# Channel attention's first group taken into the drain of the sublayer before it, and rows turned ahead of a chunk's last products

## The chip, the cores and the metric

The kernel runs on one core of a Trainium2 chip. The metric is device time in microseconds. A core has five engines with queues of their own[...]: TensorE (PE; its weight loads are shown as PEld), VectorE (DVE), ScalarE (ACT), GpSimd (POOL) and SyncE (SP), which here issues the transfers.

## The reference, cut to what matters

Four decoder layers run one after another over 64 sequences of 64 rows of 256 numbers, with a second stream `ctx` of the same shape. Each layer has an attention, a cross attention and a feed-forward sublayer, and after each comes a layer norm of the sum with what went in. The change touches the first layer and the edge to the second:

```
# first sublayer: causal attention, 16 heads of 16 that share one key and one value head
# second: channel attention (q = x, k = v = ctx), softmax over the channels of q
scaled = jnp.einsum('bsd,bse->bde', q, k) * scale        # scale = 1/16
attn = jax.nn.softmax(scaled, axis=1)
out = jnp.einsum('bde,bse->bsd', attn, v)
# third: feed-forward with 8-bit weights, hidden size 704
W = (wq - 128) * scale[:, None]
out = qlinear(silu(qlinear(x, gate)) * qlinear(x, up), down)
# second layer, first sublayer: needs the sum of 16 blocks of Wo (128 rows each)
```

## The kernel before, in words

The 4096 rows stand in eight groups of four tiles of 128 rows (`n_groups` = 8, `TG` = 4). `X[g]` holds a group's rows, `CT[g]` the transposed `ctx`; both stay on the chip. Layers are methods, called in turn by `run`; each opens its pools of on-chip buffers and closes them at its end. SP issues all loads (`load`, L327). The weights use a ring of eight buffers (`weight`), so that a load into a buffer waits for the last use of what was in it: `l1a` takes the place of the first sublayer's weights.

Within `manual_schedule` the program text fixes the order on PE, ACT, DVE and POOL. Outside it, and on SP always, a scheduler places the instructions.

`l0_attn` is the first sublayer. Its loop (`for i in range(n + 4)`) is a software pipeline over the 32 tiles. In step i come: `ended` for tile i-4 (sum with the residual L605, statistics L606 and L607, at a group's end rstd L228 and its power on POOL L230); `scores` of tile i (mask and products L539 and L544, maximum L553, subtraction L554); `probabilities` of tile i-1 (sum L563, reciprocal L564, division on POOL L565); `values` of tile i-3 (products L584, ScalarE's copy `ot` L589); one of four `parts` that prepare the next group (row turning with copies L488; keys and values L493 to L514; two query projections L493 with L530); `exponentials` of tile i (L558); `turned` for tile i-2 (transposes L236, copies L574); a piece of an earlier group's normalization, `behind` (L614, L618); `output` of tile i-3 (L595). The transposes of `turned` and the banks of the parts share two PSUM banks (tag `tr`); the scores have one buffer of four banks. The values v of a group are also exchanged between partition halves by two small transfers, vs<-v (L516), before POOL fills `vbd` with them (L526); POOL does this, and adds the bias to x (L521), in the query parts.

`l0_both` holds the other two sublayers. The feed-forward weights are loaded as integers and made into floats on DVE (L698). Each of eight chunks (one group) has HC = 6 units of 128 hidden columns. In unit u come `hidden` (gate and up products L795, Silu L797, product L798), `behind` (normalization L712, L714), then, for the tile of channel attention that the table `at` names, `divided` (reciprocal L757, division on POOL L762) and `scores` (products L738, maximum L742, scaling L743, exponentials L748), `down` for unit u-2 (L809), `values` for u-2 (L772, sum and statistics L725 to L727), and at a chunk's end `turn` of the next group's rows (transposes L785, copies L786: ScalarE the first half, VectorE the second). `at` gives tile (g, t) the unit 6(g-1)+t-2, so the loop starts at u = -8: group 0's four tiles run with no chunk beside them. `turn` and `hidden` share three PSUM banks (tag `gu`).

`l1_attn` loads the next weights; two sums over `l1_wo` (L868, L869, and their sum L870) stand in the text at its head.

## Time and profile before

| | |
|---|---|
| median of three runs | 4527.38 us (4523.95 to 4527.45) |
| profiled execution, own time | 4522.86 us |
| its span (first to last instruction) | 4521.2 us |
| granted TensorE clock, mean | 0.962 |
| first sublayer | until about 219.4 us of the span |
| group 0's channel attention | 219.4 to 252.6 us |
| first product of the first chunk | 260.58 us |
| last product of the last chunk | 619.5 us |
| the other layers | from there to 4521.2 us |

A profile is one execution, so sums are made against 4522.86 us. In rows of a timeline the columns are start, duration, engine, line and operation, out<-in, shape and count, and in brackets how long the engine had been idle and what released it. A row of waits names who waited for whom: microseconds in total, times, the longest. A row of stretches gives each engine's busy time, the granted clock, and the transfers' share.

### The profile page before, as it was taken

To read this page: it belongs to the slowest core of one execution; us is meant where nothing else is said; L and a number is where in the kernel's file an instruction comes from. 1 tells how busy PE (TensorE), PEld (TensorE's weight loads), DVE (VectorE), ACT (ScalarE), POOL (GpSimd) and SP (SyncE) were. 2 spreads that over 40 slices of the span, in tenths; PEclk is the share of its full clock that TensorE was granted. 3 is DMA by queue.
4 is the path that set the end of the run, shared out by engine and by line. 5 is a ranking of instruction groups with operands and counts; after the bars stand their busy time and mean duration, and the time that the engine had idled before them with its cause. 6 is when DMAs were issued, how large, how long until landed. Compare 5 with 4: busy or idle time off the path is not lost. (4 is left out here: it accounts for less than half of the span.)

```text
span 4521.2 us, 73893 instructions
## 1 busy us (share of the span) xinstructions
PE 4119.8 (91%) x28796; PEld 2664.4 (59%) x28816; DVE 3089.4 (68%) x6215; ACT 2020.6 (45%) x3669; POOL 1477.0 (33%) x1498
## 2 busy tenths in 40 slices
PE   8889988989988999839999999999979999999898
PEld 5644555666665555525666666666646666666566
DVE  6743435888765577767777777777756777777676
ACT  4645533766623566534444444444423332233343
POOL 4411111142331111105555555555523333333111
PEclk9989997999999999969999999999989999999999
DMA  4000011333300000011111111111220000000000
GB/s 142 13 21 2 3 42 33 64 80 71 75 1 21 1 1 1 10 47 27 26 29 28 26 29 24 29 29 27 59 63 10 10 10 10 10 10 13 6 16 17
DMA packets 99685, 128.26 MB, mean 28 GB/s; under 512 B 14916, under 2 KB 72452, under 8 KB 97928
## 3 DMA queue, kind: packets, MB, share of 16 engines
q1 hardware_dynamic: 99336, 123.53, 10.9%
q8 instruction: 228, 3.74, 0.4%
q14 instruction: 121, 0.99, 0.1%
HBM read 61.87 MB, written 19.42 MB: 18 GB/s over the span
## 5 line engine op out<-in xcount | busy, mean ns | idle before, releaser
L230 POOL TENSOR_TENSOR hrq<-hrq,neg_half 128x4 f32<-128x4 f32 x256 | 271.0, 1058 | 510.9 <-DVE hrq L228 510.8
L230 POOL TENSOR_TENSOR rstd<-rstd,neg_half 128x4 f32<-128x4 f32 (+1 forms) x168 | 148.4, 883 | 677.5 <-DVE rstd L228 595.1
L1054 DVE TENSOR_REDUCE mc<-sq 128x2 f32<-128x512 f32 x512 | 317.6, 683 | 68.3 <-PE sk L1052 66.2
L1060 ACT ACTIVATE e<-sk 128x512 f32<-128x512 f32 x512 | 265.8, 607 | 117.7 <-PE sk L1052 114.0
L230 POOL TENSOR_TENSOR hrk<-hrk,neg_half 128x4 f32<-128x4 f32 x160 | 187.9, 1174 | 290.0 <-DVE hrk L228 279.5
L1049 PE MATMUL sq<-l1x 32*128 32x256 f32 x2048 | 280.8, 412 | 1.6 <-DVE mc L1054 1.6
L1052 PE MATMUL sk<-l1x 32*128 32x256 f32 x2048 | 258.0, 399 | 0.0
L1556 PE MATMUL p<-l3a_wq,xt 128*128 128x512 f32 x512 | 244.4, 600 | 9.9 <-DVE v L217 9.9
L1556 PE MATMUL p<-l3x_wq,xt 128*128 128x512 f32 x512 | 236.2, 605 | 13.7 <-DVE k L1865 13.5
L1556 PE MATMUL p<-l3a_wk,xt 128*128 128x512 f32 x512 | 247.1, 605 | 0.0
L1049 PEld LDWEIGHTS sq<-l1x 32*128 32x128 f32 x2048 | 212.4, 197 | 55.5 <-issue 22.7
L1946 PE MATMUL acc<-l3x_wo,yt 128*128 128x256 f32 x1024 | 238.0, 385 | 0.7 <-ACT yt L215 0.7
L1556 PE MATMUL p<-l3a_wv,xt 128*128 128x512 f32 x512 | 234.4, 600 | 0.8 <-DVE k L217 0.4
L1763 PE MATMUL acc<-l3a_wproj,yt 128*128 128x256 f32 x1024 | 232.5, 380 | 0.0
L1763 PEld LDWEIGHTS acc<-l3a_wproj,yt 128*128 128x128 f32 x1024 | 194.8, 191 | 53.1 <-issue 29.2
L1946 PEld LDWEIGHTS acc<-l3x_wo,yt 128*128 128x128 f32 x1024 | 189.3, 190 | 28.3 <-ACT yt L215 0.9
L1052 PEld LDWEIGHTS sk<-l1x 32*128 32x128 f32 x2048 | 191.8, 190 | 7.0 <-issue 2.9
L1857 ACT ACTIVATE sq<-q 128x512 f32<-128x512 f32 x128 | 80.7, 631 | 206.5 <-DVE q L1865 153.9
L1556 PEld LDWEIGHTS p<-l3x_wq,xt 128*128 128x128 f32 x512 | 97.0, 195 | 125.2 <-issue 114.9
L1747 POOL TENSOR_TENSOR hry<-hry,neg_half 128x8 f32<-128x8 f32 x64 | 106.3, 1661 | 193.1 <-DVE hry L1743 193.1
L236 PEld LDWEIGHTS qT<-ident,q 128*128 128x128 f32 x1024 | 119.1, 141 | 77.2 <-issue 64.5
L1088 PE MATMUL ret<-e,vt 128*32 128x256 f32 x2048 | 140.0, 389 | 17.5 <-DVE mc L1054 16.6
(383 smaller groups left out, 10244.6 us busy)
## 6 DMA issues: line engine op xcount, KB each, us to landing
vs<-v SPq DMA_DIRECT2D x320, 128.0 KB
x<-in_x SPq DMA_DIRECT2D x8, 512.0 KB
ct<-in_ctxT SPq DMA_DIRECT2D x8, 512.0 KB
cn<-in_ctx SPq DMA_DIRECT2D x8, 512.0 KB
l1x<-in_ctx SPq DMA_DIRECT2D x128, 32.0 KB
l1x_x<-x SPq DMA_DIRECT2D x8, 512.0 KB
l1x<-l1x_x SPq DMA_DIRECT2D x128, 32.0 KB
l1x_r<-r SPq DMA_DIRECT2D x128, 32.0 KB
```

The lines of the kernel that those rows point to most:

```text
L230: nc.gpsimd.tensor_tensor(out, out, self.neg_half[:, :n], ALU.pow)
L236: self.nc.tensor.transpose(ps[:, j * P : (j + 1) * P], blk, self.ident)
L1049: nc.tensor.matmul(ps[:, n, :], x_[rows, j, part], c_[rows, j, :], start=True, stop=True)
L1052: nc.tensor.matmul(ps[:, n, :], c_[rows, j, part], x_[rows, j, :], start=True, stop=True)
L1054: nc.vector.tensor_reduce(mc[new % 2][:, ra + k, 2 * j : 2 * j + 2], ps, AX.X, ALU.max, negate=True)
L1060: nc.scalar.activation(es[rb + k], ps, AF.Exp, scale=scale)
L1088: nc.tensor.matmul(ret[32 * r : 32 * r + 32, :], vt[i % 2][:, lc, 4 * r + j, :], es[r][:, lc, :], start=lc == 0, stop=lc == 1,)
L1556: self.nc.tensor.matmul(ps, lhs(c), w(c, cols), start=c == 0, stop=c == 1 and bias is None)
L1747: nc.gpsimd.tensor_tensor(r, r, self.neg_half[:, :8], ALU.pow)
L1763: nc.tensor.matmul(acc[:, :D], yts[h % 2][:, h // 2, :], wp[n // 8][:, (n % 8) * D : (n % 8 + 1) * D], start=n == 0, stop=n == 15,)
L1857: nc.scalar.activation(sq, x, AF.Square)
L1946: nc.tensor.matmul(acc[:, :D], yts[h % 2][:, h // 2, :], wo[n // 8][:, (n % 8) * D : (n % 8 + 1) * D], start=n == 0, stop=n == 15,)
```

## The change

1. The functions of channel attention become a method, `channel_attention`, whose buffers the caller gives; the sum with statistics becomes `tile_sum`, the normalization `group_end`. The work of one tile is the same.
2. `l0_attn` loads `ctx` (`self.context(g)`, eight loads of 512 KB) at its own head. Its loop has two more steps, and runs the four tiles of group 0's channel attention in steps 32 to 37, in buffers of the first sublayer.
3. In that loop `turned` stands ahead of the parts and of `exponentials`, in every step.
4. In `l0_both`, group 1's tiles are at u = -1 to 2 (before: -2 to 1), the loop starts at u = -1, and `turn(0)` stands ahead of it. At a chunk's end `turn` stands in front of `down` and `values`, and VectorE makes both copies.
5. The loads for the next layer are issued in `l1_weights`, called in `l0_both`, and the two sums over `l1_wo` stand at u = 36 and u = 39.

On SP's queue the order of the eight `cn` loads and of the four vs<-v transfers of groups 0 and 1 is exchanged: the loads come first.

```
+    def tile_sum(self, state, g, t, z, a, b):
+        if t == 0:
+            state[g, "mv"] = self.smallp.tile([P, TG, 2], F32, tag="bnmv", name="bnmv", bufs=4)
+        st = self.smallp.tile([P, 6], F32, tag="bnst1", name="bnst1", bufs=4)
+        nc.vector.tensor_tensor(z[:, t, :], a, b, ALU.add)
+        nc.vector.bn_stats(st, z[:, t, :])
+        nc.vector.bn_aggr(state[g, "mv"][:, t, :], st)
+
+    def group_end(self, state, g, x, z, parts=1):
+        rstd, nb = self.small(TG, "rstd", bufs=4), self.small(TG, "nmr", bufs=4)
+        self.rsqrt(rstd, mv[:, :, 1], 1.0, 1e-5)
+        def apply(ts):
+            if ts[0] == 0:
+                nc.vector.scalar_tensor_tensor(nb, mv[:, :, 0], -1.0, rstd, ALU.mult, ALU.mult)
+            for i in ts:
+                nc.scalar.activation(
+                    x[:, i, :], z[:, i, :], AF.Identity, bias=nb[:, i : i + 1], scale=rstd[:, i : i + 1]
+                )
+        n = TG // parts
+        return [lambda i=i: apply(range(i * n, i * n + n)) for i in range(parts)]
+
+    def channel_attention(self, state, p_tile, vt_tile, z_tile, s_banks, o_bank):
...
...
     def l0_attn(self, ctx):
...
+        self.cns = [self.context(g) for g in range(self.n_groups)]
+        next_scores, next_divided, next_values = self.channel_attention(
...
-            for i in range(n + 4):
+            for i in range(n + TG + 2):
                 behind = ends.pop(0) if ends else None
-                if i >= 4:
+                if 4 <= i <= n + 3:
                     ended(*tiles[i - 4], state.pop((i - 4, "ps")))
                 if i < n:
...
                     state[i, "s"] = scores(g, t)
+                elif i < n + TG:
+                    next_scores(0, i - n)
                 if 1 <= i <= n:
                     probabilities(state[i - 1, "s"])
+                elif n < i <= n + TG:
+                    next_divided(0, i - n - 1)
                 if 3 <= i <= n + 2:
                     state[i - 3, "o"] = values(*tiles[i - 3], state.pop((i - 3, "pt")))
+                if 2 <= i <= n + 1:
+                    state[i - 2, "pt"] = turned(state.pop((i - 2, "s")))
                 if parts:
                     parts.pop(0)()
                 if i < n:
                     exponentials(state[i, "s"])
-                if 2 <= i <= n + 1:
-                    state[i - 2, "pt"] = turned(state.pop((i - 2, "s")))
                 if behind:
                     behind()
                 if 3 <= i <= n + 2:
                     state[i - 3, "ps"] = output(*tiles[i - 3], state.pop((i - 3, "o")))
+                if i >= n + 2:
+                    ends.extend(next_values(0, i - n - 2))
...
     def l0_both(self, ctx):
...
         def turn(g):
             xt = wk.tile([P, 2, NTOK], F32, tag="xt", name="xt")
-            for c, copy in enumerate((nc.scalar.copy, nc.vector.tensor_copy)):
+            for c in range(2):
...
-                copy(xt[:, c, :], ps)
+                nc.vector.tensor_copy(xt[:, c, :], ps)
...
-        at = {HC * (g - 1) + t - 2: (g, t) for g, t in tiles}
+        at = {HC * (g - 1) + t - (1 if g == 1 else 2): (g, t) for g in range(1, self.n_groups) for t in range(TG)}
+        self.l1_weights()
...
-            for u in range(min(at), len(units) + 2):
+            turn(0)
+            for u in range(-1, len(units) + 2):
...
                 if u in at:
                     scores(*at[u])
+                if u >= 0 and (u + 1) % HC == 0 and (u + 1) // HC < self.n_groups:
+                    turn((u + 1) // HC)
                 if u >= 2:
                     down(*units[u - 2])
                 if u - 2 in at:
-                    values(*at[u - 2])
-                if (u + 1) % HC == 0 and (u + 1) // HC < self.n_groups:
-                    turn((u + 1) // HC)
+                    ends.extend(values(*at[u - 2]))
+                if u in (HC * 6, HC * 6 + 3):
+                    self.l1_output_weight(u == HC * 6)
...
+    def l1_weights(self):
+        w = self.weight("l1a")
...
+    def l1_output_weight(self, first):
+        wo, half, raw = self.l1w[2:]
+        if first:
+            nc.vector.tensor_reduce(wo, raw[0], AX.X, ALU.add)
+        else:
+            nc.vector.tensor_reduce(half, raw[1], AX.X, ALU.add)
+            nc.vector.tensor_tensor(wo, wo, half, ALU.add)
```

More of the change, by code (lines that the diff above doesn't have):

```diff
@@ L433, in constants @@
             keep(rows, [[8, 4]], 7, -1, 0.0)
+    def tile_sum(self, state, g, t, z, a, b):
+        nc = self.nc
+        if t == 0:
[5 more added lines that the diff above has]
+    def group_end(self, state, g, x, z, parts=1):
+        nc, mv = self.nc, state.pop((g, "mv"))
+        rstd, nb = self.small(TG, "rstd", bufs=4), self.small(TG, "nmr", bufs=4)
[9 more added lines that the diff above has]
+        return [lambda i=i: apply(range(i * n, i * n + n)) for i in range(parts)]
@@ new lines, in channel_attention, with scores, divided, values @@
+    def channel_attention(self, state, p_tile, vt_tile, z_tile, s_banks, o_bank):
+        nc = self.nc
+        half = lambda b: slice(b * S, (b + 1) * S)
+        scale = 1.0 / 16.0
+        def scores(g, t):
+            x, cn = self.X[g], self.cns[g]
+            if t == 0:
+                state[g, "z"] = z_tile()
+            ps = s_banks()
+            for e in range(2):
+                for b in range(2):
+                    nc.tensor.matmul(
+                        ps[:, b, e, :], cn[half(b), t, e * P : (e + 1) * P], x[half(b), t, :], start=True, stop=True
+                    )
+            nb, sm = self.small(4, "nb4"), self.small(4, "sm4x")
+            nc.vector.tensor_reduce(nb, ps, AX.X, ALU.max, negate=True)
+            nc.vector.tensor_scalar_mul(nb, nb, scale)
+            p = p_tile()
+            for b in range(2):
+                for e in range(2):
+                    i = 2 * b + e
+                    nc.scalar.activation(
+                        p[:, b, e, :], ps[:, b, e, :], AF.Exp, bias=nb[:, i : i + 1], scale=scale,
+                        accum_out=sm[:, i : i + 1],
+                    )
+            state[g, t] = p, sm
+        def divided(g, t):
+            p, sm = state[g, t]
+            nc.vector.reciprocal(sm, sm)
+            vt = vt_tile()
+            src = self.CT[g][:, :, t * P : (t + 1) * P].rearrange("p e (b s) -> p b e s", b=2)
+            sums = sm.rearrange("p (b e) -> p b e", b=2)
+            for b in range(2):
+                nc.gpsimd.tensor_tensor(
+                    vt[:, b], src[:, b], sums[:, b].unsqueeze(2).broadcast_to([P, 2, S]), ALU.mult
+                )
+            state[g, t] = p, vt
+        def values(g, t):
+            p, vt = state.pop((g, t))
+            ps = o_bank()
+            for e in range(2):
+                for b in range(2):
+                    nc.tensor.matmul(ps[half(b), :D], vt[:, b, e, :], p[:, b, e, :], start=e == 0, stop=e == 1)
+            z = state[g, "z"]
+            self.tile_sum(state, g, t, z, ps[:, :D], self.X[g][:, t, :])
+            return self.group_end(state, g, self.X[g], state.pop((g, "z"))) if t == TG - 1 else []
+        return scores, divided, values
@@ L600, in ended @@
             xb, z = groups[g][3:]
-            if t == 0:
-                groups[g, "mv"] = self.smallp.tile([P, TG, 2], F32, tag="bnmv", name="bnmv", bufs=4)
-            mv = groups[g, "mv"]
-            st = self.smallp.tile([P, 6], F32, tag="bnst1", name="bnst1", bufs=4)
-            nc.vector.tensor_tensor(z[:, t, :], ps[:, :D], xb[:, t, :], ALU.add)
-            nc.vector.bn_stats(st, z[:, t, :])
-            nc.vector.bn_aggr(mv[:, t, :], st)
-            if t < TG - 1:
-                return
-            rstd, nb = self.small(TG, "rstd", bufs=4), self.small(TG, "nmr", bufs=4)
-            self.rsqrt(rstd, mv[:, :, 1], 1.0, 1e-5)
-            def shifts():
-                nc.vector.scalar_tensor_tensor(nb, mv[:, :, 0], -1.0, rstd, ALU.mult, ALU.mult)
-            def apply(t0):
-                for i in (t0, t0 + 1):
-                    nc.scalar.activation(
-                        self.X[g][:, i, :], z[:, i, :], AF.Identity, bias=nb[:, i : i + 1], scale=rstd[:, i : i + 1]
-                    )
-            ends.extend([shifts, lambda: apply(0), lambda: apply(2)])
+            self.tile_sum(groups, g, t, z, ps[:, :D], xb[:, t, :])
+            if t == TG - 1:
+                ends.extend(self.group_end(groups, g, self.X[g], z, 2))
         ends = []
@@ L626, in l0_attn @@
         n = len(tiles)
+        four = lambda a: a.rearrange("p r i k -> p (r i k)").rearrange("p (b e d) -> p b e d", b=2, e=2)
+        self.cns = [self.context(g) for g in range(self.n_groups)]
+        next_scores, next_divided, next_values = self.channel_attention(
+            {},
+            lambda: four(wk.tile([P, 4, 4, S], F32, tag="s", name="s", bufs=4)),
+            lambda: wk.tile([P, 4, P], F32, tag="pt", name="pt", bufs=4)[:, :2].rearrange("p b (e s) -> p b e s", e=2),
+            lambda: wk.tile([P, TG, D], F32, tag="z", name="z", bufs=2),
+            lambda: self.psum.tile([P, 4, 512], F32, tag="s", name="s", bufs=1)[:, :2].rearrange(
+                "p b (e d) -> p b e d", e=2
+            ),
+            lambda: self.bank("o", tag="ot", bufs=1),
+        )
         E = mybir.EngineType
@@ L676, in l0_both @@
         wk = ctx.enter_context(self.tc.tile_pool(name="l0b", bufs=2, reuse_waits="tile"))
-        cns = [self.context(g) for g in range(self.n_groups)]
-        half = lambda b: slice(b * S, (b + 1) * S)
-        scale = 1.0 / 16.0
         ws = []
@@ L703, in l0_both @@
         state, ends = {}, []
-        def ended(g, z):
-            mv = state.pop((g, "mv"))
-            rstd, nb = self.small(TG, "rstd", bufs=4), self.small(TG, "nmr", bufs=4)
-            self.rsqrt(rstd, mv[:, :, 1], 1.0, 1e-5)
-            def apply():
-                nc.vector.scalar_tensor_tensor(nb, mv[:, :, 0], -1.0, rstd, ALU.mult, ALU.mult)
-                for i in range(TG):
-                    nc.scalar.activation(
-                        self.X[g][:, i, :], z[:, i, :], AF.Identity, bias=nb[:, i : i + 1], scale=rstd[:, i : i + 1]
-                    )
-            ends.append(apply)
@@ L720, in sums @@
-        def sums(g, t, z, ps):
-            if t == 0:
-                state[g, "mv"] = self.smallp.tile([P, TG, 2], F32, tag="bnmv", name="bnmv", bufs=4)
-            st = self.smallp.tile([P, 6], F32, tag="bnst1", name="bnst1", bufs=4)
-            nc.vector.tensor_tensor(z[:, t, :], ps, self.X[g][:, t, :], ALU.add)
-            nc.vector.bn_stats(st, z[:, t, :])
-            nc.vector.bn_aggr(state[g, "mv"][:, t, :], st)
-        def scores(g, t):
-            x, cn = self.X[g], cns[g]
-            if t == 0:
-                state[g, "z"] = wk.tile([P, TG, D], F32, tag="z", name="z", bufs=3)
-            ps = self.psum.tile([P, 2, 2, D], F32, tag="s", name="s", bufs=1)
-            for e in range(2):
-                for b in range(2):
-                    nc.tensor.matmul(
-                        ps[:, b, e, :], cn[half(b), t, e * P : (e + 1) * P], x[half(b), t, :], start=True, stop=True
-                    )
-            nb, sm = self.small(4, "nb4"), self.small(4, "sm4x")
-            nc.vector.tensor_reduce(nb, ps, AX.X, ALU.max, negate=True)
-            nc.vector.tensor_scalar_mul(nb, nb, scale)
-            p = wk.tile([P, 2, 2, D], F32, tag="p", name="p", bufs=3)
-            for b in range(2):
-                for e in range(2):
-                    i = 2 * b + e
-                    nc.scalar.activation(
-                        p[:, b, e, :], ps[:, b, e, :], AF.Exp, bias=nb[:, i : i + 1], scale=scale,
-                        accum_out=sm[:, i : i + 1],
-                    )
-            state[g, t] = p, sm
@@ L754, in divided @@
-        def divided(g, t):
-            p, sm = state[g, t]
-            nc.vector.reciprocal(sm, sm)
-            vt = wk.tile([P, 2, 2, S], F32, tag="vt", name="vt", bufs=3)
-            src = self.CT[g][:, :, t * P : (t + 1) * P].rearrange("p e (b s) -> p b e s", b=2)
-            sums_ = sm.rearrange("p (b e) -> p b e", b=2)
-            for b in range(2):
-                nc.gpsimd.tensor_tensor(
-                    vt[:, b], src[:, b], sums_[:, b].unsqueeze(2).broadcast_to([P, 2, S]), ALU.mult
-                )
-            state[g, t] = p, vt
@@ L767, in values @@
-        def values(g, t):
-            p, vt = state.pop((g, t))
-            ps = self.bank("o", tag="o", bufs=1)
-            for e in range(2):
-                for b in range(2):
-                    nc.tensor.matmul(ps[half(b), :D], vt[:, b, e, :], p[:, b, e, :], start=e == 0, stop=e == 1)
-            z = state[g, "z"]
-            sums(g, t, z, ps[:, :D])
-            if t == TG - 1:
-                ended(g, state.pop((g, "z")))
+        scores, divided, values = self.channel_attention(
+            state,
+            lambda: wk.tile([P, 2, 2, D], F32, tag="p", name="p", bufs=3),
+            lambda: wk.tile([P, 2, 2, S], F32, tag="vt", name="vt", bufs=3),
+            lambda: wk.tile([P, TG, D], F32, tag="z", name="z", bufs=3),
+            lambda: self.psum.tile([P, 2, 2, D], F32, tag="s", name="s", bufs=1),
+            lambda: self.bank("o", tag="o", bufs=1),
+        )
@@ L817, in down @@
             for t in range(TG):
-                sums(g, t, z, acc[t // 2][:, t % 2, :])
-            ended(g, z)
-        tiles = [(g, t) for g in range(self.n_groups) for t in range(TG)]
+                self.tile_sum(state, (g, 1), t, z, acc[t // 2][:, t % 2, :], self.X[g][:, t, :])
+            ends.extend(self.group_end(state, (g, 1), self.X[g], z))
         units = [(g, i) for g in range(self.n_groups) for i in range(HC)]
-        at = {HC * (g - 1) + t - 2: (g, t) for g, t in tiles}
+        at = {HC * (g - 1) + t - (1 if g == 1 else 2): (g, t) for g in range(1, self.n_groups) for t in range(TG)}
+        self.l1_weights()
         E = mybir.EngineType
         with self.tc.manual_schedule(engines={E.PE, E.Activation, E.DVE, E.Pool}):
-            for u in range(min(at), len(units) + 2):
+            turn(0)
+            for u in range(-1, len(units) + 2):
                 behind = ends.pop(0) if ends else None
@@ L839, in l0_both @@
                 if u - 2 in at:
-                    values(*at[u - 2])
-                if (u + 1) % HC == 0 and (u + 1) // HC < self.n_groups:
-                    turn((u + 1) // HC)
+                    ends.extend(values(*at[u - 2]))
+                if u in (HC * 6, HC * 6 + 3):
+                    self.l1_output_weight(u == HC * 6)
             for part in ends:
                 part()
+    def l1_weights(self):
+        ins, DH = self.ins, 128
+        w = self.weight("l1a")
+        wkk = w[:, 0:256].rearrange("p (c n) -> p c n", c=2)
+        wvv = w[:, 256:512].rearrange("p (c n) -> p c n", c=2)
+        self.load(wkk, ins["l1_wk"].rearrange("(c p) n -> p c n", p=P))
+        self.load(wvv, ins["l1_wv"].rearrange("(c p) n -> p c n", p=P))
+        raw = []
+        for i in range(2):
+            r = self.weight(f"l1_wo{i}").rearrange("p (h n) -> p h n", h=8)
+            self.load(r, ins["l1_wo"][i * 8 * DH : (i + 1) * 8 * DH, :].rearrange("(h p) n -> p h n", p=P))
+            raw.append(r.rearrange("p h n -> p n h"))
+        self.l1w = wkk, wvv, w[:, 512:768], w[:, 768:1024], raw
+    def l1_output_weight(self, first):
+        nc = self.nc
+        wo, half, raw = self.l1w[2:]
[4 more added lines that the diff above has]
+            nc.vector.tensor_tensor(wo, wo, half, ALU.add)
     def l1_attn(self, ctx):
@@ L852, in l1_attn @@
         wk = self.pool(ctx, "l1a", 2)
-        w = self.weight("l1a")
-        wkk = w[:, 0:256].rearrange("p (c n) -> p c n", c=2)
-        wvv = w[:, 256:512].rearrange("p (c n) -> p c n", c=2)
-        wo = w[:, 512:768]
-        self.load(wkk, ins["l1_wk"].rearrange("(c p) n -> p c n", p=P))
-        self.load(wvv, ins["l1_wv"].rearrange("(c p) n -> p c n", p=P))
-        raw = []
-        for i in range(2):
-            r = self.weight(f"l1_wo{i}")
-            self.load(
-                r.rearrange("p (h n) -> p h n", h=8),
-                ins["l1_wo"][i * 8 * DH : (i + 1) * 8 * DH, :].rearrange("(h p) n -> p h n", p=P),
-            )
-            raw.append(r)
-        half = w[:, 768:1024]
-        nc.vector.tensor_reduce(wo, raw[0].rearrange("p (h n) -> p n h", h=8), AX.X, ALU.add)
-        nc.vector.tensor_reduce(half, raw[1].rearrange("p (h n) -> p n h", h=8), AX.X, ALU.add)
-        nc.vector.tensor_tensor(wo, wo, half, ALU.add)
+        wkk, wvv, wo = self.l1w[:3]
         bk, bv = self.column("l1_bk"), self.column("l1_bv_col")
```

## The prediction, made before the changed kernel ran

> **What bounds the kernel now.** I read the page's busy shares first, then busy time by stretches of the first layer (the only part whose instructions change place), then the waits of its second half, then single timelines at four places.

> ```profile
> ## 1 busy us (share of the span) xinstructions
> PE 4119.8 (91%) x28796; PEld 2664.4 (59%) x28816; DVE 3089.4 (68%) x6215; ACT 2020.6 (45%) x3669; POOL 1477.0 (33%) x1498
> ```

> TensorE is busy 91% of the span: a step pays only where TensorE waits. By stretches (us; PE, PEld, DVE, ACT, POOL busy; granted clock; DMA share, GB/s):

> ```profile
> 125.00:150.00 25.00, 23.99 (x367) 17.32 (x366) 20.82 (x33) 15.85 (x28) 11.91 (x11) 1.00 0.01 3
> ...
> 220.00:260.00 40.00, 19.09 (x94) 11.24 (x90) 21.36 (x47) 15.93 (x58) 7.03 (x12) 0.69 0.11 29
> ...
> 351.00:396.00 45.00, 41.35 (x157) 21.32 (x156) 17.66 (x45) 25.98 (x55) 5.18 (x9) 0.96 0.01 4
> ```

> The first sublayer's loop is full of TensorE work (24 of 25 us); channel attention of group 0 is a chain with TensorE busy 48% at clock 0.69; a chunk (45 us) loses about 4. The waits of the second half name it:

> ```profile
> PE gate L795 <- ACT xt L786: 21.9, 8, 3.7
> PE s L738 <- ACT p L748: 3.7, 2, 3.5
> ```

> Eight chunks, and the first product of each waits for ScalarE's copy of the turned rows. One boundary, from the timelines of PE, ACT and DVE:

> ```profile
> 397.50 1.04 PE L785 MATMUL xt<-ident,x 128*128 128x128 f32 x8
> 402.19 3.34 PE L795 MATMUL gate<-xt,l_wg 128*128 128x512 f32 x4 [3.66 <-ACT xt L786]
> 405.32 2.26 PE L795 MATMUL up<-xt,l_wu 128*128 128x512 f32 x4
> ...
> 401.54 0.59 ACT L786 COPY xt<-xt 128x512 f32<-128x512 f32 x1
> ...
> 396.94 1.19 DVE L742 TENSOR_REDUCE nb<-s 128x4 f32<-128x1024 f32 x1
> ...
> 398.57 0.69 DVE L786 COPY xt<-xt 128x512 f32<-128x512 f32 x1 [0.24 <-PE xt L785]
> ```

> The ACT copy takes 0.59 but stands behind four exponentials and their table load (398.43 to 401.54). VectorE's copy was done at 399.26. The products after the stall take 3.34 and 2.26, elsewhere 1.98 and 1.88 at full clock.

> **Gain 1, boundaries.** Chunks 1 to 5 stall 3.65, 3.66, 3.66, 3.66, 3.66 and lose 1.64, 1.74, 1.75, 0, 1.74 to the slower clock behind it: 25.1 us. With the change: scores end 395.67; four transposes, 0.5; the next four need the bank of the last gate, read by Silu until 396.22, so they end at 396.75 (0.1 waited); the down products (1.83) now lie behind them and end at 398.6. VectorE finishes its maximum at 398.33 and copies to 399.0 and 399.6. The gate starts with the first half, at 399.05: a wait of 0.45. Left: 0.55 a boundary, 2.7 in five. Gain 22.4. What is late next is VectorE's maximum ahead of the copies. Chunk 6 waits 0.24 plus hand-over: gain 0.4.
> [...] by the queues the 0.1 buys 3 us. I take the queues. [...]

> **Gain 2, the drain.** In before, the last subtraction of the first sublayer ends at 207.59 and the first chunk's gate starts at 260.58, up at 264.15. After, by before's durations: scores 1.1, maximum and scaling behind queued VectorE work, exponentials to 213.4; each next tile waits its round, ot copy 0.4, output 0.9, scores 1.1, maximum and scaling 1.65, exponentials 1.9 (about 5.95): 219.35, 225.2. Tile 3 also stands behind the last output, the first values and two sums (3 x 1.05): 233.3. Reciprocal and division 1.2, values 1.1, sums and rstd 1.3, power and shift 1.5, four applies 2.1 : 240.5. Turning and copying 1.8, group 1's maximum 1.3, dequantizing wg 1.9 and wu 1.9: gate 245.6, up 247.5. That is 16.6 earlier; some 8 us of this chain is TensorE's and the stretch it replaces ran at 0.69, so I take 2 off: 14.6. Bounds 11 and 16.6.
> In this the turning of group "-1" at 228.07 (the condition also held at u = -7) vanishes; it lay beside exponentials and is worth nothing by itself. The scale loads still wait for the last output (SP, behind l1a), and land some 10 us before they are used.

> **Chunk 0 and the moved sums.** Before:

> ```profile
> 288.87 3.68 DVE L869 TENSOR_REDUCE l1a<-l_wo 128x256 f32<-128x2048 f32 x1 [2.98 <-DMA l_wo<-in_l_wo]
> ...
> 301.55 2.08 PE L738 MATMUL s<-x,cn 64*128 64x256 f32 x8 [3.52 <-ACT p L748]
> ```

> The sum of l1_wo waits for its load in VectorE's queue; group 1's normalization and exponentials stand behind, and TensorE stalls 3.52, 1.2 more at the boundary, and loses 2.7 of clock: 7.4. After, the sums lie at u = 36 and 39, 3.7 and 4.1 us, in units of 6.9 and 6.4 us where VectorE has 3 to 5 of other work; only h products with two units of slack stand behind. I cost them at nothing (1 each if that slack is gone). But group 1 enters with one tile instead of two, so one more scores (1.1), and the loop exponentials, table load, Silu, product, maximum, table load takes 7.4 where TensorE has 4.7 to 6: waits 2.2, 1.6, 1.4; and turn(1) waits for group 1's applies, 2.1. Sum 8.4 against 7.6: 0.8 lost. With gain 2: 13.8.

> **Loss 1, the start.** In the changed order SP issues eight cn loads (0.5 MB each) before the first vs transfer, not after. The SP, POOL and PE timelines:

> ```profile
> 21.43 0.42 SPq L327 DMA_DIRECT2D l_ob<-in_l_ob  x1
> 22.84 4.42 SPq L516 DMA_DIRECT2D vs<-v  x4
> 28.15 9.19 SPq L327 DMA_DIRECT2D cn<-in_ctx  x8
> ...
> 31.77 2.34 POOL L521 TENSOR_TENSOR xb<-x,l_ob 128x1024 f32<-128x1024 f32 x1 [24.97 <-DMA vs<-v]
> ...
> 35.01 1.90 POOL L565 TENSOR_TENSOR s<-s,sm 128x1024 f32<-128x1024 f32 x1
> ...
> 36.97 1.97 PE L236 MATMUL pt<-ident,s 128*128 128x128 f32 x8 [9.15 <-POOL s L565]
> ```

> GpSimd waits for l_ob and vs, then fills vbd, then divides; TensorE stands 9.15 us. l_ob, issued behind seven open loads, took 10.3 us[...]. So vs waits for 4.2 MB more; at the 345 GB/s of 17 to 50 us, 12.2: it lands near 43.9 instead of by 31.8. The two vs copies and the last v copy follow (0.8), division at 44.9 instead of 35.01: 9.9 lost. Lower end: a small transfer overtakes, 0; upper end 12.2. I take 9.9 because l_ob is the nearest row. Turning tile 0 also moves ahead of the query projection at i = 2, which lay in that stall: its 1.8 comes out. Loss 11.7.

> **Loss 2, `turned` ahead of the parts, 25 tiles.** PE and POOL timelines:

> ```profile
> 115.48 0.66 PE L236 MATMUL pt<-ident,s 128*128 128x128 f32 x4 [0.34 <-ACT qT L530]
> ...
> 116.56 1.90 POOL L565 TENSOR_TENSOR s<-s,sm 128x1024 f32<-128x1024 f32 x1 [0.78 <-DVE sm L564]
> ...
> 122.31 1.90 POOL L565 TENSOR_TENSOR s<-s,sm 128x1024 f32<-128x1024 f32 x1 [3.03 <-ACT pt L574]
> ```

> Now the projection's bank is freed by ScalarE after the first half of `turned` (gaps 0.44, 0.44, 0.51, and 0 in the keys part). After, the projection waits for the first pt copy: 0.43 in each of four parts, so 0.3 lost a group. And `turned` needs the division: it is ready 6.28 after the values begin one tile earlier (117.99 to 124.27). TensorE's work until then is 6.37 with a projection between, 8.2 with keys, but 5.46 with the row turning: a wait of 0.8. Together 1.15 a group, 6.25 groups: 7.2. Ends: 2 (only the banks) and 31 (below).

> **Sum.** 22.4 + 0.4 + 13.8 - 11.7 - 7.2 = 17.7 us. The profiled execution took 4522.86 (span 4521.2), so 4505.2; the runs' median is 4.5 higher, so 4509.7.

> **Rivals.** (a) vs overtakes the cn loads, or lands early: loss 1 falls to 1.8, 4500. For it: a 16 KB transfer; against it: l_ob's 10.3. (b) VectorE is too late at the boundaries, so half the stall and the clock loss stay: gain 1 is 11, 4521. For it: its maximum ends only 0.3 before the down products; against it: the first copy suffices for the gate's first half. (c) Slower: the division decides in every tile, not one in four. `turned` stands directly behind it with 0.1 us to spare in projection tiles; if the wait is 0.8 plus 0.43 in each of 25 tiles, loss 2 is 31 and the time 4533. It decides from 1.0 us a tile (7.2 + 17.7, over 25).

> **How the numbers follow.** Forecast 0.60 (own range 4499 to 4519), (a) 0.14, (b) 0.15, (c) 0.11. A measurement of this kernel tells about 0.2% (9 us) from no change: below 4518.3 is faster, above 4536.4 slower. The forecast, nearly all of it, (a) and a part of (b) are faster: 0.75; the rest of (b) and most of (c): 0.19; 0.06 slower. Range 4495 to 4525.

> **What would show it.** vs landing at 43 to 45 and division of tile 0 near 45; PE waits of 0.4 on ACT pt and 0.8 on POOL s between 50 and 200; first gate near 266, 6 us after its old 260.58, because the two losses (18.9) come before gain 2's 13 to 15, and everything won after that; boundary gaps of 0.5 on DVE xt with gates at 1.98; the waits for ACT xt gone. The forecast is wrong if TensorE still stalls 2 us or more at boundaries, or if the loop's tiles grow by over 1 us.

## The result, and the profile after

The changed kernel takes 4507.9 us (median of 7 runs, 4501.6 to 4513.1), the kernel before beside it 4524.0 (7 runs, 4522.8 to 4527.6): a ratio of 0.9962, with a 95% interval of 0.9950 to 0.9973. That is 16.1 us faster; 17.7 were predicted, and a time of 4509.7. The profiled execution took 4513.13 us (span 4511.4). Up to the first products of the second layer (kv) it is 13.7 us ahead of the kernel before, and in the layers behind, whose instructions did not change, it gives 4.0 back.

How those 13.7 came about is seen by cutting both profiles at five events: POOL's division of tile 0, VectorE's last subtraction (tile 31), the first gate, the second chunk's first gate, the last chunk's. All numbers are lengths in us.

```
                               predicted   before    after   difference
start, to the division of tile 0    +9.9    35.01    44.42     +9.4
loop, to the last subtraction       +9.0   172.57   182.19     +9.6
drain, to the first gate           -13.0    52.99    43.17     -9.8
chunk 0                             -0.8    48.79    48.31     -0.5
chunks 1 to 6                      -22.8   274.53   252.18    -22.3
last chunk, to kv                    0      43.17    43.06     -0.1
sum                                -17.7   627.07   613.34    -13.7
```

The prediction counts the drain's 14.6 to the first `up` product (264.15 to 247.5, less 2). By its own times the gate in front of it comes 15.0 earlier, 13.0 with the 2 taken off; the other 1.6 lie behind the first gate, which would run at full clock, and so in the row of chunk 0 (+0.8 less 1.6). Five terms are within 0.6 us of the forecast; the drain is 3.2 off, and the first gate, foretold near 266, comes at 269.78. Now the lines. First the stretches (us; PE, PEld, DVE, ACT, POOL busy; granted clock; DMA share; GB/s) of the drain, of chunk 0 and of one later chunk:

```profile
228.00:270.00 42.00, 25.69 (x197) 15.39 (x186) 19.23 (x49) 16.57 (x51) 8.83 (x12) 0.80 0.10 28
269.70:318.00 48.30, 43.29 (x160) 21.60 (x161) 21.18 (x48) 29.11 (x65) 4.79 (x11) 0.93 0.07 22
360.00:405.00 45.00, 44.36 (x175) 23.65 (x175) 20.01 (x50) 28.32 (x62) 5.04 (x10) 1.00 0.07 24
```

The later chunk is full: 44.36 of 45 us, clock 1.00 (before: 41.35 at 0.96). The drain is not: clock 0.80. The waits of TensorE in the second half of the layer:

```profile
PE s L479 <- ACT p L489: 3.7, 2, 2.6
PE gate L808 <- DVE l_wg L777: 2.1, 1, 2.1
PE gate L808 <- DVE xt L799: 1.6, 5, 0.3
```

The 21.9 us for ScalarE's xt have become 1.6 for VectorE's. One boundary, from the timeline of PE:

```profile
400.52 1.89 PE L822 MATMUL acc<-l_wd,hid 128*128 128x256 f32 x8
402.74 1.99 PE L808 MATMUL gate<-xt,l_wg 128*128 128x512 f32 x4 [0.32 <-DVE xt L799]
```

A gap of 0.32 and a gate of 1.99, where there were 3.66 and 3.34. The start, from the timelines of SP and of POOL:

```profile
22.71 13.03 SPq L327 DMA_DIRECT2D cn<-in_ctx  x8
35.86 3.17 SPq L600 DMA_DIRECT2D vs<-v  x4
```

```profile
43.64 0.52 POOL L610 COPY vbd<-vs 64x64 f32<-64x64 f32 x2 [9.81 <-DMA vs<-v]
...
44.42 1.90 POOL L649 TENSOR_TENSOR s<-s,sm 128x1024 f32<-128x1024 f32 x1
```

vs is issued at 35.86 instead of 22.84, lands at 43.6, and the division follows at 44.42 instead of 35.01. And the loop's new waits, TensorE, 55 to 205 us:

```profile
PE prep L577 <- ACT pt L658: 5.5, 19, 0.3
PE pt L236 <- POOL s L649: 3.3, 6, 0.7
```

Both are the ones foretold, a little shorter each (0.29 for 0.43; five of the six divisions 0.61 or 0.65 for 0.8). A group of four tiles takes 24.90 us instead of 23.76: 1.14 more, where 1.15 were foretold.

### The profile page after: what moved, and what is told of

It is laid out like the page before. It is cut to its first block, busy times and chain, and to the rows that moved or that the text cites. A ratio compares the mean times of both kernels' runs of the same rounds, so it can differ in the third digit from the quotient of the medians.

```text
span 4511.4 us, 73874 instructions
## 1 busy us (share of the span) xinstructions
PE 4118.9 (91%) x28808; PEld 2662.9 (59%) x28808; DVE 3091.6 (69%) x6222; ACT 2018.8 (45%) x3662; POOL 1474.4 (33%) x1498
## 5 line engine op out<-in xcount | busy, mean ns | idle before, releaser
L1580 PE MATMUL p<-l3x_wq,xt 128*128 128x512 f32 x512 | 238.2, 609 | 13.9 <-DVE k L1889 13.7
L236 PEld LDWEIGHTS qT<-ident,q 128*128 128x128 f32 x1024 | 119.1, 141 | 77.3 <-issue 64.6
```

What stands on the lines that cost most here:

```text
L236: self.nc.tensor.transpose(ps[:, j * P : (j + 1) * P], blk, self.ident)
L1580: self.nc.tensor.matmul(ps, lhs(c), w(c, cols), start=c == 0, stop=c == 1 and bias is None)
```

## The experiments

Five questions: whether both losses come from where the working put them (four runs), what it is that gains at the boundaries (three), what the moved sums are worth (one), what the drain still leaves (three), and whether the clock is what a stall costs beyond itself (one). The lengths of the five stretches in each profiled execution, in us; start, loop, drain, chunk 0, chunks 1 to 6, and when kv begins:

```
                   start    loop   drain  chunk 0  chunks 1-6      kv
before             35.01  172.57   52.99    48.79      274.53  627.07
after              44.42  182.19   43.17    48.31      252.18  613.34
e1_vs_first        35.45  182.19   40.35    48.31      252.19  601.56
e2_turned_back     45.05  173.37   41.28    48.31      252.20  603.28
e3_both            35.00  172.60   40.37    48.33      251.87  591.24
e8_vs_act_queue    34.38  193.89   41.24    48.32      252.22  613.12
e4_copies_only     34.83  172.39   52.28    42.27      251.86  596.80
e5_front_only      34.72  172.73   52.97    48.34      274.13  625.97
e6_turn_both       34.30  172.28   52.29    42.56      251.31  595.81
e7_sums_only       34.31  172.71   52.99    45.05      276.17  624.40
e9_dequant_early   34.13  172.50   38.06    47.09      252.13  586.97
e10_two_ahead      36.00  172.23   38.69    44.20      251.94  586.13
e11_both_on_top    34.29  173.45   40.58    40.48      251.94  583.82
e12_filled         34.17  172.91   53.01    46.37      269.44  618.96
```

**e1: the loads of cn behind the first four transfers of vs (groups 0 and 1; not twelve, as the expectation has it).**

```
-        self.cns = [self.context(g) for g in range(self.n_groups)]
+                if i == 2:
+                    self.cns = [self.context(g) for g in range(self.n_groups)]
```

> The changed kernel with the eight loads of cn issued behind the twelve loads of vs of tiles 0 to 2 on SyncE's queue, instead of ahead of them. First theory (the loads of vs of tile 0 are served behind the 512 KB loads of cn in the order in which they were issued): the division of tile 0 goes back from 44.4 us to 35 us, everything up to the first gate comes some 9.4 us earlier, and the time is about 9.4 us below that of the changed kernel, near 4498 us. Rival (the division is late for another reason, x landing at 31 us or the bandwidth that all the loads share): it stays near 44 and the time near 4508 us. The first three scores would then wait for cn if cn came later than they do: a wait on cn at the first scores of a group of more than 1 us would show that.

4498.88 us, ratio 0.9947 (0.9934 to 0.9959). The start is back at 35.45, 9.0 us earlier, and no scores of group 0 wait for cn. It is the place of vs behind the cn loads that makes the start late; whether vs waits there to be served, as the expectation has it, or to be issued, e1 does not tell.

**e2: `turned` behind the exponentials again, but for the last six tiles (26 to 31; the expectation says four).**

```
-                if 2 <= i <= n + 1:
+                if n - TG <= i <= n + 1:
                     state[i - 2, "pt"] = turned(state.pop((i - 2, "s")))
...
                     exponentials(state[i, "s"])
+                if 2 <= i < n - TG:
+                    state[i - 2, "pt"] = turned(state.pop((i - 2, "s")))
```

> The changed kernel with the transposes of the probabilities (pt) of the tiles up to 27 behind the exponentials again, as before, and ahead of the parts only in the last four. First theory (the two short waits, 0.29 us on ACT pt and 0.61 us on POOL s, come of the new place and of nothing else): both go in the steady loop, the first gate comes some 7 to 9 us earlier, and the time is about 4499 us. Rival (the loop is bound by the division or the clock and the waits only change their place): the rate of the loop stays, and the time stays near 4508 us.

4502.77 us, ratio 0.9955 (0.9943 to 0.9968). The loop is 8.8 us shorter (182.19 to 173.37), and the first gate comes 10.1 earlier: the place of `turned` is the loss. Of that the median shows 3 us by the ratios, 5 by the times; the layers behind kv scatter by more than such differences, so the events up to kv carry these verdicts.

**e3: both.**

> The changed kernel with both edits: cn issued behind the first loads of vs, and pt turned behind the exponentials up to tile 27. If the two losses are separate and add up, the last subtraction comes back from 226.6 us to about 208 us, the first gate to about 251 us, and the time is about 19 us below the changed kernel, near 4489 us, 35 us below the kernel before. If they are the same wait seen twice, it is no more than 10 us below, near 4498 us.

4491.2 us, ratio 0.9931 (0.9917 to 0.9944). Start 35.00, loop 172.60, as before the change; the first gate is at 247.97, 21.8 us before that of the changed kernel (e1 alone 11.8, e2 alone 10.1). They add up: two losses. The waits of e3's loop, 55 to 205 us:

```profile
PE pt L236 <- ACT qT L614: 4.1, 12, 0.3
PE pt L236 <- POOL s L649: 2.9, 2, 1.7
```

Twelve short waits for a bank stand where the changed kernel has nineteen, and the division is waited for twice, not six times.

**e8: vs issued on ScalarE's queue.**

```
-                    nc.sync.dma_start(out=vs[half(b)], in_=v[half(1 - b)])
+                    nc.scalar.dma_start(out=vs[half(b)], in_=v[half(1 - b)])
```

> The changed kernel with the loads of vs issued on ScalarE's queue instead of SyncE's, at the same place of the program. First theory (vs waits only because it stands behind cn in one queue): vs of tile 0 lands within 4 us of its issue, the division of tile 0 is near 36 to 37 us, and the time is some 7 to 9 us below the changed kernel, near 4500 us. Rival (the transfers share one bandwidth, and vs is late whatever its queue): the division stays near 43 to 44 us and the time near 4508 us. [...]

4512.43 us, ratio 0.9979 (0.9970 to 0.9988): no better than the changed kernel, though the start is 34.38: vs is no longer what the division waits for. What it had waited for in the changed kernel is its turn to be issued on SP. It was issued 13.0 us later than before and was there 7.8 us after its issue (before, at most 8.9). e8 itself does not settle whether bandwidth matters too, for ScalarE issues group 0's vs at 12.91, ahead of the first cn load (24.89). What I had not seen is the price on ScalarE. Its timeline in e8, and below it the same place in e1:

```profile
138.05 1.45 ACT L584 ACTIVATE kbd<-prep,kbp,pair 128x512 f32<-128x512 f32 x2 [1.59 <-PE prep L577]
139.99 1.12 ACTq L600 DMA_DIRECT2D vs<-v  x2
141.16 1.06 ACT L642 ACTIVATE s<-s 128x1024 f32<-128x1024 f32 x1 [1.66 <-DVE z L443]
```

```profile
133.04 1.45 ACT L584 ACTIVATE kbd<-prep,kbp,pair 128x512 f32<-128x512 f32 x2 [1.59 <-PE prep L577]
134.38 1.05 ACT L642 ACTIVATE s<-s 128x1024 f32<-128x1024 f32 x1
```

The two issues take 1.12 us, and stand in ScalarE's order with the wait for v's copy in front of them, so the exponentials behind come 1.8 us later after `kbd`. From 83 us on a group takes 26.5 us instead of e1's 24.9, and 28.2 in the two that hold an interval of half clock (at 103 and 158 us); that is most of the 11.7 us by which the loop is longer than e1's. In the whole sublayer there are 16 such issues, of 0.55 us in the median. What ScalarE's queue spares vs is the place behind the 13.03 us of issues in SP's row above.

**e4, e5, e6: what gains at the boundary.** e4 is the kernel before with only this edit:

```
-            for c, copy in enumerate((nc.scalar.copy, nc.vector.tensor_copy)):
+            for c in range(2):
...
-                copy(xt[:, c, :], ps)
+                nc.vector.tensor_copy(xt[:, c, :], ps)
```

e5 is the kernel before with only `turn` moved in front of `down` and `values`; e6 has both edits.

> The kernel before with VectorE making both copies of xt, and the turn left behind the down products. First theory (the stall of 3.66 us and the clock that follows it come of ScalarE's copy, which stands behind the exponentials; with VectorE the copies follow the transposes at once): the gate waits about 0.9 to 1.3 us at each of the five boundaries on DVE xt, granted clock back at 1.00, some 3.9 to 4.5 us a boundary, 18 to 21 us in all: about 4504 us. Rival (the order in front of the down products does it): within 2 us of 4524 us.

> The kernel before with the turn in front of the down products of a chunk's last step, and its two copies on ScalarE and VectorE as before. First theory (the stall is fixed by ScalarE's copy behind the exponentials of the last step): the gates of the next chunk begin where they did or at most 1 us earlier, since the down products now lie behind the transposes and take 1.9 us of the wait; the clock may stay up since the idle gap is shorter than 3.66 us, which would be worth up to 1.7 us at four of the boundaries. So 4515 to 4524 us. Rival (the place does it, whatever engine copies): the stall goes and the time is near 4504 us.

> The kernel before with the turn in front of the down products and both copies on VectorE, and nothing else of the change. First theory: the gain of the six boundaries alone, 22.3 to 22.8 us, gate waiting 0.3 us on DVE xt at the granted clock 1.00: about 4501 us, so below the changed kernel, of which the other parts together lose some 7 us. Rival (the turns gain less without the early gate): near 4508 us or above.

e4: 4493.52 us, ratio 0.9932 (0.9919 to 0.9944). e5: 4522.44, 0.9994 (0.9986 to 1.0002), no difference. e6: 4494.09, 0.9934 (0.9920 to 0.9947). So VectorE's copy is all of it, and the place of the turn nothing. The gate of the same boundary in e4, PE, right behind the turn:

```profile
386.53 1.98 PE L795 MATMUL gate<-xt,l_wg 128*128 128x512 f32 x4 [0.45 <-DVE xt L786]
```

and what TensorE waits for in e5 between 300 and 560 us:

```profile
PE gate L795 <- ACT xt L786: 18.6, 6, 3.5
```

In e5 the start of the gate is set by ScalarE's queue, whatever TensorE does meanwhile. e4 also gained more than expected, and that in chunk 0, which is 6.5 us shorter. The stretches of chunk 0 in e4 and, below, in the kernel before:

```profile
259.50:301.70 42.20, 38.43 (x152) 19.74 (x152) 23.11 (x39) 22.31 (x49) 5.00 (x10) 1.00 0.18 54
```

```profile
260.50:309.30 48.80, 43.85 (x152) 22.47 (x152) 22.69 (x37) 24.13 (x52) 4.99 (x10) 0.87 0.16 47
```

The same 152 products take 38.43 us at clock 1.00 instead of 43.85 at 0.87, though a wait for ScalarE's p of 3.0 is still there (3.5 before). Of the 6.5 us, 5.4 are TensorE's time for the same work, and so the clock.

The size of e4 matters for the whole change. By itself it is some 14 us faster than the changed kernel, and e3, the changed kernel with both losses taken out, has nearly the same ratio (0.9931 against 0.9932; in the profiles kv comes 5.6 us earlier). Taking group 0 into the drain shortens the drain (52.28 in e4, 40.37 in e3), but chunk 0, which then begins with one tile scored and not two, is longer (42.27 and 48.33). Only in e9 to e11 below does the move pay more: kv comes 9.8, 10.7 and 13.0 us before e4's.

**e7: the sums of l1_wo at u = 36 and 39 in the kernel before**, with their loads issued ahead of the chunks (the edit is item 5 of the change).

> The kernel before with the two sums of l1's output weight moved from the head of layer 1 into the last chunk of the channel attention, after the steps that the changed kernel uses, their loads issued ahead of the first chunk; nothing else of the change. The sums stood in chunk 0's or layer 1's way for no more than 0.4 us in my sum. First theory: within 3 us of 4524 us if the place of VectorE's sums is covered on both sides; up to 6 us faster if layer 1 begins earlier by the sums (3.5 us) and by the clock that the gap costs (2.7 us). Rival: the loads, issued ahead, hold back those of the first chunks' weights, and the time is 2 us or more above 4524 us.

4523.67 us, ratio 0.9998 (0.9990 to 1.0006): no difference. Chunk 0 is 3.7 us shorter, and the parts are those of the prediction: the stall of 3.52 is down to 0.2, and the same 152 products take 41.19 us at clock 0.94 instead of 43.85 at 0.87. But the gate behind chunk 0 now waits 3.65 us for ScalarE's xt, where it had waited 1.21, so 2.4 of the gain stay there. Chunks 1 to 6 are 1.6 longer. That is not the sums' new place, chunk 6, which is 1.0 shorter (40.50 against 41.54), but chunk 5, 2.6 longer, with two intervals of half clock at its head where the kernel before had none. So the stall went, ScalarE's copy and the clock took a good part of it back, and the 2.7 us by which kv is earlier are too few for the medians to tell. A cost of the loads that I feared does not show.

**e9, e10, e11: what the drain leaves**, each on e3. e9 writes the dequantizations into VectorE's order, e10 scores group 1's first tile ahead of the first turn, e11 does both (l_wg then behind the scores):

```
+            scores(1, 0)              # e10, e11; at[...] is t - 2 for every g
+            steps[0]()                # e9, e11: dequantize l_wg
             turn(0)
+            steps[1]()                # e9, e11: l_wu
...
-                if u in at:
+                if u in at and u > -2:    # e10, e11
                     scores(*at[u])
+                if u == -1:
+                    steps[2]()        # e9, e11: l_wd
```

> The changed kernel with cn behind the first loads of vs and pt turned behind the exponentials (4491.2 us as measured), and besides the dequantizations of the three l0 weights written into the order of the drain: l_wg in front of the first turn of the rows, l_wu behind its copies, l_wd behind the scaling of nb. First theory (part of the gain of the drain that is missing lies in VectorE's order there: the first gate waits 2.1 us on DVE l_wg, and the scaling of nb stands 5.2 us behind the dequantizations, so that the exponentials of group 1 and with them the next two scores come late, 1.1 and 2.6 us waited): the wait on l_wg goes, the one of 1.1 goes and the one of 2.6 stays, and the time falls by 3 to 4 us, to about 4488 us. Rival (the clock decides, and the early gate only runs at half of it): less than 1 us.

> The same base (4491.2 us), with the scores of the first tile of group 1 put in front of the first turn of the rows, where TensorE stands 3.3 us waiting for ScalarE's rows, so that group 1 enters chunk 0 with two tiles scored as in the kernel before. First theory (chunk 0 takes 48.3 us instead of 42.3 as in the kernel with only the copies moved, since one more scores and its waits stand in it, and the turn of chunk 1 waits for group 1's rows): chunk 0 falls to 43 us or below, and the time by 4 to 6 us, to about 4486 us. Rival (chunk 0's loss is the clock, which comes back at a fixed rhythm): less than 2 us.

> Both edits on that base: the dequantizations early and the scores of group 1's first tile in front of the first turn. If they add up, the first gate starts near 245 us, chunk 0 takes 41 to 43 us, and the time is 7 to 10 us below the base, near 4483 us, 41 us below the kernel before and 25 below the changed one. If the clock takes the place of the waits that go, 4487 us or more.

e9: 4485.3 us, 0.9913 (0.9898 to 0.9928). e10: 4483.65, 0.9909 (0.9894 to 0.9923). e11: 4481.69, 0.9906 (0.9889 to 0.9922), the best version: 44 us below the kernel before beside it. The medians of the three lie within each other's intervals; in the profiles kv comes 4.3, 5.1 and 7.4 us earlier than in e3, so the edits don't add up. e9 went as expected: the wait on l_wg is gone, that of 1.1 is down to 0.2, that of 2.6 is left, and the next tile's scores wait 1.55 that they did not wait before. In e10 chunk 0 fell to 44.2, not to 43: its first gate took 3.13 us, part of it at half clock, where 1.98 is the time at full, and waits of 2.5 and 1.55 for p are left in it. What e11's timeline of PE has ahead of the first gate, and the gate:

```profile
239.65 1.14 PE L479 MATMUL s<-x,cn 64*128 64x256 f32 x8
...
246.32 2.08 PE L479 MATMUL s<-x,cn 64*128 64x256 f32 x8 [0.48 <-ACT p L489]
248.32 2.93 PE L813 MATMUL gate<-xt,l_wg 128*128 128x512 f32 x4
```

The scores of one tile take 1.14 at full clock, those of the next 2.08 at half. The first gate comes 3.6 us after e9's, which runs in 1.98; but chunk 0, at 40.48, is 6.6 us shorter. The expected 245 us for the gate was not reached; chunk 0, expected at 41 to 43, came out below that.

**e12: the stalls filled with products that nobody reads**, in the kernel before:

```
                     turn((u + 1) // HC)
+                    ps = self.bank("o", tag="o", bufs=1)
+                    for j in range(20):
+                        t = j % TG
+                        nc.tensor.transpose(ps[:, t * P : (t + 1) * P], self.X[0][:, t, :P], self.ident)
```

> The kernel before, with twenty transposes that nobody reads written into the stall of each chunk boundary, behind the turn of the rows; nothing is left out. First theory (what a boundary loses besides its stall is the clock, and the clock falls at the end of a 3.41 us window in which TensorE was busy less than about half: in the traces so far always below 0.40 and never above 0.65): 20 x 0.13 us = 2.6 us of work keep every such window above 0.65, the stalls stay as long as they were with the work in them (the gate still begins 4.7 us behind the turn), no boundary loses the clock, and chunks 1 to 5 take 1.6 to 1.8 us less at four of the five boundaries: 274.5 us from the second chunk's first gate to the last chunk's falls to 267 to 268 us, and the time by about 7 us, to near 4517 us. Rival (the longer products behind a stall come of something else, such as weights or rows that come late): they stay, and the time is 4524 us or more.

4516.44 us, ratio 0.9985 (0.9979 to 0.9992): with 180 transposes more, and no other change, the kernel is 6.7 us faster. One boundary of it, PE, and the stretch of a chunk:

```profile
393.71 2.35 PE L846 MATMUL o<-ident,x 128*128 128x128 f32 x20
397.52 1.98 PE L795 MATMUL gate<-xt,l_wg 128*128 128x512 f32 x4 [1.47 <-ACT xt L786]
```

```profile
351.00:396.00 45.00, 44.06 (x188) 24.86 (x188) 19.60 (x48) 25.60 (x54) 5.93 (x11) 1.00 0.01 4
```

The gate still starts 4.7 us behind the turn's begin, for the same reason, but takes 1.98 and not 3.34, and the clock is 1.00 from boundary to boundary. Chunks 1 to 6 take 269.4 us, 5.1 less than before; 267 to 268 were expected, and the rest is the last boundary, which has no stall to fill and where the 20 transposes come on top.

## Why the prediction was right, and where it was not

**Boundaries, 22.8 predicted, 22.3 measured.** The chain was right: ScalarE's copy behind the exponentials (all its rows were turned by 398.54, and it began at 401.54), VectorE's a row later, a wait of 0.45 us foretold and 0.32 found. That no clock is lost behind so short a wait was an estimate of mine; the gate behind it took 1.99 us, and the stretch that holds it ran at 1.00. One step was idle: the working had the down products cover the copies, and e4 against e6 shows that this place gives nothing that can be measured (42.38 us a chunk in both). VectorE's copies are soon enough by themselves (in e4 the gate above waits 0.45 us).

**Loss 1, the start, 9.9 predicted, 9.4 measured**, and shown by e1. The direction of the argument, vs behind the loads that SP has ahead of it, is borne out by SP's rows and by e1. Its size was argued from bytes (4.2 MB at 345 GB/s, 12.2 us), and the row shows where the time really went: SP needs 13.03 us to issue the eight loads, and vs is issued 13.0 us later; part of that had been slack. Why an issue took that long is not shown. Nor is it shown that transfers are served in the order of their issue, which was my estimate: l_ob's 10.3 us is an upper bound, since POOL's row at 31.77 names vs as what came last. That the two figures are close is in part luck.

**Loss 2 with the 1.8 of the start, 9.0 predicted, 9.6 measured**, and shown by e2 and e3.

**Gain 2, the drain, 13.0 predicted to the first gate, 9.8 measured (to `up` 14.6 and 10.8): the step that failed.** The order of the chain came out as written, and its durations hold where the clock is full. What was too small is the term "some 8 us of this chain is TensorE's and the stretch it replaces ran at 0.69, so I take 2 off": up to `up`, 5.8 of the 16.6 came off in the profiled execution and 2.8 in e1. The links of the chain, in us from the end of the last subtraction (the forecast is the prediction's, before the 2 come off):

```
                               forecast   after     e1     e2
exponentials of tile 0 end         5.8      5.7    5.7    5.7
of tile 1                         11.8     13.1   11.7   13.6
of tile 2                         17.6     20.8   17.8   19.7
of tile 3                         25.7     30.9   27.9   27.9
last apply                        32.9     37.8   34.8   35.8
first gate                        38.0     43.2   40.4   41.3
first up                          39.9     45.8   42.8   43.8
```

These parts of the three kernels have the same instructions in the same order. The first round of TensorE behind tile 0, in the changed kernel and, below, in e1:

```profile
232.66 1.57 PE L679 MATMUL o<-l0a,ot 128*128 128x256 f32 x4 [1.41 <-ACT ot L673]
234.15 2.08 PE L479 MATMUL s<-x,cn 64*128 64x256 f32 x8
```

```profile
223.68 1.13 PE L679 MATMUL o<-l0a,ot 128*128 128x256 f32 x4 [1.42 <-ACT ot L673]
224.75 1.13 PE L479 MATMUL s<-x,cn 64*128 64x256 f32 x8
```

At full clock a round takes 6.0 us, as foretold (5.95). Where an interval of half clock falls into it, output and scores take up to 2.08 instead of 1.13, and the round takes 7.4 to 7.9: two rounds in the changed kernel, one in e2, none in e1. So with the third, foretold at 8.1: 8.25 in e2 at full clock, 10.1 in the other two at half. The two chains together filled TensorE for 25.69 of 42 us only, and that did not keep the clock (0.80 on the mean). Which rounds are hit differs between executions of one order (drains of 40.35, 41.28, 40.37 and 41.24 us in e1, e2, e3 and e8), so by my estimate, 43.17 less these four, some 2 to 3 us of what is missing depend on when the drain begins, and an edit far away shifts that.

**Chunk 0, 0.8 gained predicted by these cuts (0.8 lost, less the 1.6 of the first gate), 0.5 measured**: right by size, and the first gate and its `up` start 2.65 us apart, not 1.9. The 7.4 us put down to the sums are borne out by e7 (a stall of 3.5 and 2.7 of clock, less what returned at the boundary). What the working missed is that most of it was not the sums' alone: e4 leaves the sums, keeps a stall of 3.0, and gains 6.5, since the clock stays up. So this gain was to be had without moving the sums. The loss beside it, group 1's entry with one tile, goes when two are scored first (e10 and e11).

**The total.** Of the 17.7 the profiled execution had 13.7 at kv and 9.7 at its end; the medians give 16.1. The 4 us between kv and the end are not the change's: with the same instructions, this part takes 3888.5 to 3899.2 us in the 14 profiled executions, and goes with the time that the clock is at half in it (correlation 0.87). None of the three rivals came true: vs did not overtake, VectorE was not too late (0.32), and the division was waited for in one tile of four.

## What to carry to other kernels

As e4 shows, a copy out of PSUM (the memory that products are written to) that the next products wait for belongs on the engine whose queue is free at that moment, not on the one whose copy is shorter: 0.1 us more a copy (0.69 on VectorE, 0.59 on ScalarE) bought 3.3 us of stall and the clock (1.00 in the changed kernel's later chunk, 0.96 before). Before moving loads ahead, count what their issue takes on the queue (13.03 us for eight here) and which small transfer stands behind them. A chain that is overlapped with another must be costed at the clock that its TensorE share will get (0.80 here, where 25.69 of 42 us were filled), and as a range, since the same order hit one round in one execution and two in another.

## What the runs showed of the hardware

```
clock now   busy share of TensorE    intervals   full clock next
full        below 0.40                     364                 0
full        0.40 to 0.55                   328               187
full        0.55 to 0.65                   303               301
full        above 0.65                   14374             14369
half        below 0.75                     487                 0
half        0.75 to 0.90                   192                46
half        above 0.90                     488               466
```

Some matmul records are missing and ends are modelled, so the borders are soft. At full clock no interval filled to less than 0.40 kept it (0 of 364), and above 0.55 nearly all did (14670 of 14677); at half clock none below 0.75 brought it back (0 of 487), and 466 of 488 above 0.90 did. So in the changed kernel's drain it comes and goes: an interval filled to 0.48 is followed by one at half clock, which the slower products fill to 1.00, the clock returns, and the next, filled to 0.41, loses it again. It fits that four of the five equal stalls of 3.66 us lost the clock and one didn't: the four left intervals of 0.00, 0.14, 0.29 and 0.08, while the fifth lay across two intervals, which kept 0.49 and 0.43. Shorter gaps lose it too: in e3 one of 2.1 us ahead of the first gate and one of 2.6 in chunk 0 lost the clock at 249.1 and 262.8 us (busy shares of 0.38 and 0.28). e12 tests the cause: with the stalls filled, the gate above takes 1.98 us instead of 3.34. That the spread of the changed kernel's runs (11.6 us against 4.7) has the same cause is likely but was not tried.
